# Layer 0 of a two-layer transformer: token tiles transposed by VectorE in 32x32 blocks, with rows regrouped by transfers

## The chip, the core and the metric

The program runs on one core of a Trainium2 chip. The core has five engines that run their own instruction queues in order and wait for each other through semaphores: TensorE (PE; its weight loads are shown as PEld), VectorE (DVE), ScalarE (ACT), GpSimd (POOL) and SyncE (SP), which here only issues DMA transfers. Matrix products read from SBUF, the on-chip memory of 128 partitions, and write to PSUM, from where VectorE or ScalarE copies ("evacuates") them back to SBUF. Sixteen DMA engines move data between DRAM and SBUF. The metric is the device time of one execution in microseconds (us).

## What is computed

Two layers on 1024 tokens of 512 channels, all in float32. Each layer is attention and a feed-forward product, each followed by adding its input and a layer normalisation:

```python
x = L0_attn_x                                      # (4, 256, 512)
x = _layernorm(x + _L0_attn_ref(x, Wq, bq, Wk, bk, Wv, bv, Wo, bo))
x = _layernorm(x + _L0_ffn_ref(x, q_scales, q_vals, bias))
x = _layernorm(x + _L1_attn_ref(x, w_qkv, w_o))
x = _layernorm(x + _L1_ffn_ref(x, kernel))
```

Layer 0 has 32 query heads of 16 channels on 8 key and value heads, 4 batches of 256 positions, causal; its feed-forward weight is quantised, `W = q_scales * (q_vals - 128)` in blocks of 32, and `out = x @ W.T + bias`. Layer 1 has 32 heads of 128 channels and a distance bias.

## The kernel before

The tokens lie in eight tiles of 128 rows (`tt` 0 to 7); a batch `b` is the tiles 2b and 2b+1. A matrix product needs the channels on the partitions, so each token tile is transposed before it is used: 128 tokens x 512 channels become `[128, 4, 128]`, channel within a group of 128, group `c`, token.

Layer 0 needs this three times for each tile: the input `x` (before the projections, `project0`), the normalised `x1` (before the feed-forward product `pf`) and the normalised `x2` (for layer 1, into `x2T`; both in `tail0`). `transposed` does it with four TensorE transposes into one PSUM bank (`pt_x`, line 272) and one copy out. `evacuate` gives the copies out of PSUM to VectorE (line 102) and ScalarE (line 104) in turns.

The softmax of layer 0 runs in 64 steps `(b, qt, h, i)`: 4 batches, 2 halves of the queries (128 each; the first sees 128 keys, the second 256), and 8 groups of 4 heads. `begin0` of a step computes scores into one of two PSUM banks (`sc`, line 484, pool `ps_s0`), adds the causal mask (VectorE, line 489), takes the negated maximum (`nm`, VectorE, line 492) and the four exponentials with their sums (ScalarE, line 276); `divided` multiplies by the reciprocal of the sums on GpSimd (line 284) one step later. `transpose0`, three steps later, transposes the probabilities on TensorE (`pt`, line 299); `end0` at the end of each half multiplies by the values (`o`, line 532) and starts a `tail0`.

`run` starts one step after another and calls `fill` in each. `fill` lets every open `tail0` go on to its next `yield` and lets the projections of the next batch go on by one piece. `tail0(tt)` is: output projection `py` (line 440), sum with the input, statistics, the normalisation to `x1` (line 266), some empty `yield`s, transpose of `x1`, `pf` (line 457), sum, statistics, normalisation to `x2`, empty `yield`s, transpose of `x2`. The framework has a scheduler: the instructions on each engine come out in an order that it plans, except where `keep_in_program_order` or `issue_after` hold them. What it planned is then fixed; on the chip each engine takes its instructions in that order.

All loads but three are issued by SP, in its queue's order: first those of batch 0 and the small ones, then input tiles 2 and 3, `bo_b`, the quantised weights `qv` (1 MB) and `qs`, `wop` in eight pieces, `fb_b`, tiles 4 to 7, `table`, and the first weights of layer 1 (`load_weights1`). Eight semaphores are used in turn, so a transfer is issued when the one eight before it has landed. `feed_forward_weight` dequantises `qv` on VectorE (line 210) and transposes it (`pw`).

After layer 0, `project1` begins layer 1 with products that need tiles 0 to 3 of `x2T` (`p_k`, `p_q`, `p_v`); `token_sums` on GpSimd (lines 606 to 609) needs tiles 0 to 2 and 4 to 6 first, then 3 and 7. The weights of `p_v` (2 MB, line 724) are loaded into memory that layer 0 used until its last `py`. In layer 1 a helper `transposed_by_blocks` is already there: VectorE transposes 32x32 blocks (line 310) and transfers through DRAM put the blocks in place (lines 316 and 320, tensor `way`). It is not changed.

Of the kernel before, what the change touches and what calls it, by code (L numbers as in the profile page):

```python
# [12 lines left out]
F32 = mybir.dt.float32  # L13
I32 = mybir.dt.int32
# [6 lines left out]
P = 128  # L21
B, S, D = 4, 256, 512
NTT = B * S // P
NC = D // P
# [37 lines left out]
def block_kernel(  # L62
# [20 lines left out]
    nc = tc.nc  # L83
    slopes = [float(s) for s in alibi_slopes()]

    def pool(stack, name, bufs=1, **kw):
        return stack.enter_context(tc.tile_pool(name=name, bufs=bufs, **kw))
# [3 lines left out]
    w1 = pool(ctx, "w1", 2)  # L91
    dram = pool(ctx, "dram", 4, space=bass.MemoryType.DRAM)

    turn = [0]
    last = []

    def evacuate(dst, src):

        if not last:
            turn[0] ^= 1  # L100
        if turn[0] and not last:
            nc.vector.tensor_copy(dst, src)
        else:
            nc.scalar.copy(dst, src)  # L104


    x = []
    xf = x_in.flatten_outer_dims()
# [10 lines left out]
    x2T = const.tile([P, NC, B * S], F32, name="x2T")  # L119
# [4 lines left out]
    wa = pool(la, "wa", side="right")  # L124
    a0 = pool(la, "a0", 2, side="right")
# [7 lines left out]
    def bank_t(name):  # L133
        return ring[0].tile([P, 4, P], F32, tag=ring[1], name=name)

    def bank_m(name):
        return ps_w.tile([P, D], F32, tag="w", name=name)
# [11 lines left out]
    bo_b = wa.tile([P, D], F32, name="bo_b")  # L149
    fb_b = w0.tile([P, D], F32, name="fb_b")  # L150
    brow = wa.tile([G + 1, P], F32, name="brow")
    qv = wa.tile([P, NC, D], I32, name="qv")
    qs = wa.tile([P, NC, D // BLK], F32, name="qs")
    wf_n = qv.bitcast(F32)

    tc.keep_in_program_order(nc.scalar.dma_start(wk, Wk.rearrange("(c p) n -> p c n", p=P)))
    tc.keep_in_program_order(
# [7 lines left out]
    nc.sync.dma_start(brow[G : G + 1, :], bk.unsqueeze(0))  # L165
    nc.sync.dma_start(wv, Wv.rearrange("(c p) n -> p c n", p=P))
    nc.sync.dma_start(bv_b, bv.partition_broadcast(P))
    for tt in range(2, 4):
        nc.sync.dma_start(x[tt], xf[ts(tt, P), :])
    nc.sync.dma_start(bo_b, bo.partition_broadcast(P))  # L170
    nc.sync.dma_start(qv, q_vals.rearrange("(c p) n k -> p c (n k)", p=P))
    nc.sync.dma_start(qs, q_scales.rearrange("(c p) n -> p c n", p=P))
# [1 line left out]
    for h in range(NKV):  # L174
        nc.sync.dma_start(wop[16 * h : 16 * h + 16, :, :], wo_v[h])
    nc.sync.dma_start(fb_b, f_bias.partition_broadcast(P))
    for tt in range(4, NTT):
        nc.sync.dma_start(x[tt], xf[ts(tt, P), :])
    nc.sync.dma_start(table, dist)

# [7 lines left out]
    def bias_columns():  # L188

        pt = bank_t("pt_bias")  # L190
        nc.tensor.transpose(pt[:, 0, 0 : G + 1], brow, ident[0 : G + 1, 0 : G + 1])
        nc.vector.tensor_copy(bcol, pt[:, 0, 0 : G + 1])
# [3 lines left out]
    def query_columns():  # L196

        for i in range(G):
            ins = (nc.vector.tensor_copy, nc.scalar.copy, nc.gpsimd.tensor_copy)[min(i, 2)](
                wq[:, :, i, :].rearrange("p c (h d) -> p c h d", d=16), wq_v[:, :, i]  # L200
            )
            tc.keep_in_program_order(ins)
# [23 lines left out]
    s0 = pool(l0, "s0", 2)  # L226
# [27 lines left out]
    def norm_factors(y, name):  # L254

        st = s0.tile([P, 6], F32, tag="bn", name=f"bn_{name}", bufs=4)
        mv = s0.tile([P, 2], F32, tag="mv", name=f"mv_{name}", bufs=4)
        rs = s0.tile([P, 1], F32, tag="rs", name=f"rs_{name}", bufs=4)
        nc.vector.bn_stats(st, y)
        nc.vector.bn_aggr(mv, st)  # L260
        nc.vector.tensor_scalar(rs, mv[:, 1:2], EPS, 1.0, ALU.add, ALU.mult)
        powers.append(nc.gpsimd.tensor_tensor(rs, rs, minus_half, ALU.pow))
        return mv[:, 0:1], rs

    def normalise(dst, y, factors):
        nc.vector.tensor_scalar(dst, y, *factors, ALU.subtract, ALU.mult)

    def transposed(dst, src, name):

        pt = bank_t(f"pt_{name}")  # L270
        for c in range(NC):
            nc.tensor.transpose(pt[:, c, :], src[:, ts(c, P)], ident)
        evacuate(dst, pt)

    def exponentials(pr, sc, nm, sums, i, w):
        nc.scalar.activation(  # L276
            pr[:, i, 0:w], sc, AF.Exp, bias=nm[:, i : i + 1], accum_out=sums[:, i : i + 1]
        )
# [91 lines left out]
    def project0(b):  # L370
        xT = a0.tile([P, NC, S], F32, tag="xT", name=f"xT_{b}", bufs=1)
        qT = a0.tile([P, G, S], F32, tag="qT", name=f"qT_{b}")
        kT = a0.tile([P, 2, S], F32, tag="kT", name=f"kT_{b}")
        v = a0.tile([P, 2, 4, 64], F32, tag="v", name=f"v_{b}")
        nc.gpsimd.memset(v, 0.0)
        qkv0[b] = (qT, kT, v)
        rest = ROOM[min(b, 2)]
        for _ in range(rest[0]):
            yield True
        for j in range(2):  # L380
            transposed(xT[:, :, ts(j, P)], x[2 * b + j], f"x_{b}_{j}")
        if b == 0:
            bias_columns()
            query_columns()
        yield True
        pk = bank_m(f"pk_{b}")
        for c in range(NC):
            nc.tensor.matmul(
                pk[:, 0:S], wk[:, c, :], xT[:, c, :], start=(c == 0), stop=(c == NC - 1)
            )  # L390
        for e in range(2):
            nc.vector.tensor_scalar(
                kT[:, e, :], pk[:, 0:S], bcol[:, G : G + 1], even[:, e : e + 1], ALU.add, ALU.mult
            )
        yield True
        for i in range(G):
            for _ in range(rest[1 + i]):
                yield True
            pq = bank_m(f"pq_{b}_{i}")
            for c in range(NC):  # L400
                nc.tensor.matmul(  # L401
                    pq[:, 0:S], wq[:, c, i, :], xT[:, c, :], start=(c == 0), stop=(c == NC - 1)
                )
            nc.vector.tensor_scalar(
                qT[:, i, :], pq[:, 0:S], bcol[:, i : i + 1], 0.25, ALU.add, ALU.mult
            )
            if i > 1:
                tt = 2 * b + i - 2
                tc.keep_in_program_order(nc.gpsimd.tensor_tensor(x[tt], x[tt], bo_b, ALU.add))
            yield True  # L410
        for _ in range(rest[5]):
            yield True
        pv = bank_m(f"pv_{b}")
        for j in range(2):
            for c in range(NC):
                nc.tensor.matmul(
                    pv[:, ts(j, P)],
                    xT[:, c, ts(j, P)],
                    wv[:, c, :],
                    start=(c == 0),  # L420
                    stop=(c == NC - 1),
                )
        for e in range(2):
            nc.vector.tensor_tensor(
                v[:, :, :, 48 * e : 48 * e + 16],
                pv[:, 0 : 2 * P].rearrange("p (j r e d) -> p j r e d", j=2, e=2, d=16)[:, :, :, e],
                bv_b.rearrange("p (r e d) -> p r e d", e=2, d=16)[:, :, e]
                .unsqueeze(1)
                .to_broadcast([P, 2, 4, 16]),
                ALU.add,  # L430
            )
        yield True

    x2 = {}

    def tail0(tt, oT):

        py = bank_m(f"py_{tt}")
        for i in range(G):
            nc.tensor.matmul(py, oT[:, i, :], wop[:, i, :], start=(i == 0), stop=(i == G - 1))  # L440
        y = s0.tile([P, D], F32, tag="y", name=f"y_{tt}")
        nc.vector.tensor_tensor(y, py, x[tt], ALU.add)
        factors = norm_factors(y, f"a{tt}")
        yield True
        x1 = s0.tile([P, D], F32, tag="x1", name=f"x1_{tt}")
        normalise(x1, y, factors)
        yield True
        if tt < NTT - 1:
            yield True
            yield True  # L450
        x1T = s0.tile([P, NC, P], F32, tag="x1T", name=f"x1T_{tt}")
        transposed(x1T, x1, f"x1_{tt}")
        nc.gpsimd.tensor_tensor(x1, x1, fb_b, ALU.add)
        yield True
        pf = bank_m(f"pf_{tt}")
        for c in range(NC):
            nc.tensor.matmul(  # L457
                pf, x1T[:, c, :], wfT[:, c, :], start=(c == 0), stop=(c == NC - 1)
            )
        y2 = s0.tile([P, D], F32, tag="y", name=f"y2_{tt}")  # L460
        nc.vector.tensor_tensor(y2, pf, x1, ALU.add)
        factors = norm_factors(y2, f"b{tt}")
        yield True
        x2[tt] = xp.tile([P, D], F32, tag="x", name=f"x2_{tt}")
        normalise(x2[tt], y2, factors)
        yield True
        if tt < NTT - 1:
            yield True
            yield True
        transposed(x2T[:, :, ts(tt, P)], x2[tt], f"x2_{tt}")  # L470
        yield True

    ahead, tails = deque(), deque()
# [82 lines left out]
    def fill():  # L556
        advance_all(tails)
        advance(ahead)

    ahead.append(project0(0))  # L560
    tails.append(feed_forward_weight())
    run(
# [7 lines left out]
        more=2,  # L570
        rest=divide0,
    )
    la.close()


# [527 lines left out]
```

## Time and profile before

| | us |
|---|---|
| median of 3 runs (lowest, highest) | 961.02 (960.78, 964.9) |
| the profiled execution, its own time | 960.96 |
| its span, first to last instruction | 958.8 |
| layer 0, its first score to its last `py` | about 14 to 270 |
| PE busy in the span | 922.0 (96%) |
| DVE busy | 619.4 (65%) |
| ACT busy | 315.2 (33%) |
| POOL busy | 445.6 (46%) |
| mean granted TensorE clock | 0.992 |

Busy time counts an engine's instructions from start to end. PE's instructions are pipelined, so one that lasts 0.6 us may hold the engine for less; the next one's start tells. "Idle" comes with a releaser: whose event ended the wait. Until 36 us the DMA engines are busy with the loads; after that they are idle until the weights of layer 1 are loaded at 270 us.

### The profile page before, as it was taken

How to read it: one execution, taken by the hardware profiler on the slowest of the kernel's cores; microseconds unless marked ns; L12 is line 12 of the kernel's file. 1: busy time of each engine (PE TensorE's matmuls, PEld its weight loads, DVE VectorE, ACT ScalarE, POOL GpSimd, SP SyncE). 2: the span in 40 equal slices, each digit the busy share in tenths (PEclk: the TensorE clock that was granted, in tenths of full speed). 3: DMA queues.
4: the chain of work that ended last, by engine and by line, in shares of the span. 5: the costliest groups of instructions: out<-in, count | busy, mean ns of one | idle time of the engine just before them, and what ended most of it. 6: DMA issues, size and time to landing. Idle time of an engine off the chain costs nothing.

```text
span 958.8 us, 11377 instructions
## 1 busy us (share of the span) xinstructions
PE 922.0 (96%) x3593; PEld 554.1 (58%) x3593; DVE 619.4 (65%) x1291; ACT 315.2 (33%) x1194; POOL 445.6 (46%) x461
## 2 busy tenths in 40 slices
PE   8999999998899999999999999999999999999996
PEld 5655455553544445666666666666666666666652
DVE  4886777778533447655667666666676576666566
ACT  3674555466411003232222222212122122214441
POOL 3563553554457015445443543534543534556732
PEclk9999999999899999999999999999999999999998
DMA  8500000000020102444443353343344333432001
GB/s 242 184 1 1 0 1 1 1 1 1 1 88 22 45 0 72 128 115 126 110 135 86 112 152 99 121 125 95 117 125 111 115 83 110 126 94 69 1 34 55
DMA packets 76418, 74.45 MB, mean 78 GB/s; under 512 B 5957, under 2 KB 52678, under 8 KB 76358
## 3 DMA queue, kind: packets, MB, share of 16 engines
q1 hardware_dynamic: 75014, 72.02, 26.2%
q10 hardware_dynamic: 1344, 1.70, 0.6%
q8 instruction: 29, 0.48, 0.2%
q14 instruction: 31, 0.25, 0.1%
HBM read 49.58 MB, written 24.12 MB: 77 GB/s over the span
## 4 chain that ended last, share of the span: by engine, by line
PE 79%; POOL 9%; DVE 6%; ACT 2%; issue 1%; DMA 1%; ACTq 0%; POOLq 0%; DVEq 0%
PE p_q L632 18%; PE po L881 14%; PE sc L968 7%; PE o L1008 7%; PE p_k L632 5%; PE p_v L632 5%; PE sc L484 4%; PE pt L299 3%; PE py L440 3%; PE pf L457 3%; PE o L532 2%; PE pq L401 2%; POOL pr L284 2%; ACT pr L276 2%; PE py L842 2%; POOL x L903 2%
## 5 line engine op out<-in xcount | busy, mean ns | idle before, releaser
L276 ACT ACTIVATE pr<-sc,nm 128x256 f32<-128x256 f32 (+1 forms) x512 | 209.5, 421 | 362.2 <-DVE nm L984 277.2
L284 POOL TENSOR_TENSOR pr<-pr,sums 128x512 f32<-128x512 f32 (+1 forms) x128 | 190.4, 1489 | 231.2 <-DVE sums L281 220.9
L976 DVE SCALAR_TENSOR_TENSOR sc<-table,sc 128x128 f32<-128x128 f32 (+1 forms) x256 | 86.1, 356 | 34.7 <-PE sc L968 32.4
L276 ACT ACTIVATION_READ_ACCUMULATOR pr<-sc,nm 128x1 f32 x512 | 104.2, 203 | 0.0
L968 PEld LDWEIGHTS sc<-kT,qT 128*128 128x128 f32 x512 | 82.3, 191 | 35.1 <-issue 29.7
L968 PE MATMUL sc<-kT,qT 128*128 128x256 f32 (+1 forms) x512 | 95.0, 327 | 0.0
L1008 PE MATMUL o<-prT,v 128*128 128x512 f32 x192 | 92.9, 592 | 0.0
L310 DVE STREAM_TRANSPOSE blocks<-pr 128x512 f32<-128x512 f32 x84 | 57.6, 698 | 45.2 <-POOL pr L284 45.1
L646 DVE TENSOR_TENSOR qT<-p_q,qT 128x512 f32<-128x512 f32 x96 | 64.6, 686 | 33.6 <-PE p_q L632 32.8
L299 PE MATMUL pt<-ident,pr 128*128 128x128 f32 x432 | 64.3, 284 | 11.7 <-POOL pr L284 8.2
L299 PEld LDWEIGHTS pt<-ident,pr 128*128 128x128 f32 x432 | 50.7, 145 | 38.1 <-issue 19.9
L984 DVE TENSOR_REDUCE nm<-sc 128x2 f32<-128x512 f32 (+1 forms) x128 | 70.1, 551 | 1.5
L484 PE MATMUL sc<-kT,qT 32*128 32x256 f32 (+1 forms) x256 | 61.6, 532 | 2.8 <-ACT pr L276 2.7
L492 DVE TENSOR_REDUCE nm<-sc 128x4 f32<-128x512 f32 (+1 forms) x64 | 61.0, 954 | 1.2
L881 PE MATMUL po<-wo,so 128*128 128x256 f32 x224 | 58.0, 381 | 2.1 <-POOL so L612 2.1
L632 PE MATMUL p_q<-x2T,ws_q 128*128 128x512 f32 x128 | 59.8, 592 | 0.0
L489 DVE TENSOR_TENSOR sc<-sc,causal 128x512 f32<-128x512 f32 x64 | 44.4, 694 | 22.8 <-PE sc L484 22.5
L104 ACT COPY o<-o 128x512 f32<-128x512 f32 x29 | 17.0, 586 | 124.9 <-PE o L1008 124.9
L632 PE MATMUL p_q<-xt,ws_q 128*128 128x512 f32 x128 | 57.7, 592 | 0.0
L881 PE MATMUL po<-wo,o 128*128 128x256 f32 x224 | 57.7, 380 | 0.0
L632 PE MATMUL p_q<-x2T,wq 128*128 128x512 f32 x128 | 57.6, 592 | 0.0
L881 PE MATMUL po<-to,so 128*128 128x256 f32 x224 | 53.3, 381 | 1.0 <-POOL so L615 1.0
(155 smaller groups left out, 1410.2 us busy)
## 6 DMA issues: line engine op xcount, KB each, us to landing
way<-blocks SPq DMA_DIRECT2D x112, 128.0 KB, 2.5
prT<-way SPq DMA_DIRECT2D x28, 512.0 KB, 3.7
wq<-in_L_attn_w_qkv_dram SPq DMA_DIRECT2D x8, 1024.0 KB, 5.1
wo<-in_L_attn_w_o_dram SPq DMA_DIRECT2D x8, 1024.0 KB, 5.1
way<-blocks SPq DMA_DIRECT2D x112, 64.0 KB, 1.8
prT<-way SPq DMA_DIRECT2D x28, 256.0 KB, 2.6
wk<-in_L_attn_w_qkv_dram SPq DMA_DIRECT2D x4, 512.0 KB, 4.1
wv<-in_L_attn_w_qkv_dram SPq DMA_DIRECT2D x2, 1024.0 KB, 6.3
```

The source lines that it names most:

```text
L276: nc.scalar.activation(pr[:, i, 0:w], sc, AF.Exp, bias=nm[:, i : i + 1], accum_out=sums[:, i : i + 1])
L284: nc.gpsimd.tensor_tensor(pr[:, :, 0:w], pr[:, :, 0:w], sums.unsqueeze(2).to_broadcast([P, G, w]), ALU.mult)
L299: nc.tensor.transpose(pt[:, i, :], pr[:, i, ts(kt, P)], ident)
L484: nc.tensor.matmul(sc[:, j, :, 0:w], qT[rows, i, ts(qt, P)], kT[rows, :, 0:w], start=True, stop=True)
L492: nc.vector.tensor_reduce(nm, scf[:, :, 0:w], AX.X, ALU.max, negate=True)
L632: nc.tensor.matmul(bank, fixed, moving, start=(c == 0), stop=(c == 1))
L646: add = lambda dst, a, b: nc.vector.tensor_tensor(dst, a, b, ALU.add)
L881: nc.tensor.matmul(bank[:, ts(n, HALF)], left[:, c, :], right[:, c, :], start=(c == 0), stop=(c == 1),)
L968: nc.tensor.matmul(sc[:, m, 0:w], qT[:, 2 * j + m, b * S + qt * P : b * S + (qt + 1) * P], kT[:, b * S : b * S + w], start=True, stop=True,)
L976: nc.vector.scalar_tensor_tensor(sc[:, m, 0:w], table[:, 2 * P - w :], slopes[kv * G + 2 * j + m], sc[:, m, 0:w], ALU.mult, ALU.add,)
L984: nc.vector.tensor_reduce(nm[:, 2 * j : 2 * j + 2], sc[:, :, 0:w], AX.X, ALU.max, negate=True)
L1008: nc.tensor.matmul(o, v1[:, 2 * b + kt, ts(kv, P)], prT[:, kt].rearrange("p j h q -> p h j q"), start=(kt == 0), stop=(kt == qt),)
```

## The change

In layer 0 twenty of the twenty-four token tiles are no longer transposed by TensorE. VectorE's `transpose` turns 32x32 blocks, each within 32 partitions, so the rows have to be regrouped first. `load_regrouped` reads a tile of 128 tokens from DRAM so that partition `32a + s` gets, for the tokens `4s` to `4s + 3` and the four channel groups, the 32 channels of its block `a`: four transfers, one for each `a`, each of 512 pieces of 32 floats (128 bytes). One `transpose` of the tile, written with a stride of four tokens, then gives the same layout as before.

- Input tiles: batch 0 stays on TensorE. For batches 1 to 3, `load_batch` loads both tiles regrouped from the input in DRAM (8 transfers): batch 1 where tiles 2 and 3 were loaded, batch 2 before the plain loads, batch 3 from within `project0(2)`. The plain tiles 2 to 7, still needed for the sum, are now all loaded after `fb_b`.
- `x1` and `x2` of tiles 0 to 6: `way_out` stores the tile to DRAM after its normalisation, `way_back` loads it regrouped into one buffer and transposes it. Tile 7 stays on TensorE.
- `evacuate`: in layer 0 one copy in three goes to VectorE, then every second one as before.
- `qv` takes a buffer of the layer 1 output weights, so the second of these (`wo`, 1 MB) is loaded later.

```diff
     turn = [0]
+    shares = [3]
     def evacuate(dst, src):
         if not last:
-            turn[0] ^= 1
-        if turn[0] and not last:
+            turn[0] += 1
+        if turn[0] % shares[0] == 1 and not last:
             nc.vector.tensor_copy(dst, src)
...
-    qv = wa.tile([P, NC, D], I32, name="qv")
+    wf_n = w1.tile([P, NC, D], F32, tag="wo1", name="wf_n")
+    qv = wf_n.bitcast(I32)
...
-    for tt in range(2, 4):
-        nc.sync.dma_start(x[tt], xf[ts(tt, P), :])
+    def load_regrouped(dst, src):
+        for a in range(4):
+            nc.sync.dma_start(
+                dst[ts(a, 32)].rearrange("s j c f -> s (j c) f"),
+                src.rearrange("(s j) (c a f) -> a s (j c) f", j=4, c=NC, f=32)[a],
+            )
+    def load_batch(b):
+        rows[b] = a0.tile([P, 8, NC, 32], F32, tag="rows", name=f"rows_{b}")
+        for j in range(2):
+            load_regrouped(rows[b][:, 4 * j : 4 * j + 4], xf[ts(2 * b + j, P), :])
+    load_batch(1)
     nc.sync.dma_start(bo_b, bo.partition_broadcast(P))
...
     nc.sync.dma_start(fb_b, f_bias.partition_broadcast(P))
-    for tt in range(4, NTT):
+    load_batch(2)
+    for tt in range(2, NTT):
         nc.sync.dma_start(x[tt], xf[ts(tt, P), :])
...
+    def transposed_regrouped(dst, src):
+        ins = nc.vector.transpose(dst.rearrange("p c (s j) -> p j c s", j=4), src)
+        tc.keep_in_program_order(ins)
+    def way_out(src, name):
+        way = dram.tile([P, D], F32, tag="rows", name=f"rows_{name}")
+        nc.sync.dma_start(way, src)
+        return way
+    def way_back(dst, way, name):
+        back = s0.tile([P, 4, NC, 32], F32, tag="back", name=f"back_{name}", bufs=1)
+        load_regrouped(back, way)
+        transposed_regrouped(dst, back)
...
         for j in range(2):
-            transposed(xT[:, :, ts(j, P)], x[2 * b + j], f"x_{b}_{j}")
+            if b == 0:
+                transposed(xT[:, :, ts(j, P)], x[j], f"x_{b}_{j}")
+            else:
+                transposed_regrouped(xT[:, :, ts(j, P)], rows[b][:, 4 * j : 4 * j + 4])
+        if b == 2:
+            load_batch(3)
...
         normalise(x1, y, factors)
-        yield True
         if tt < NTT - 1:
+            way = way_out(x1, f"x1_{tt}")
+        yield True
+        if tt < NTT - 1:
             yield True
             yield True
         x1T = s0.tile([P, NC, P], F32, tag="x1T", name=f"x1T_{tt}")
-        transposed(x1T, x1, f"x1_{tt}")
+        if tt < NTT - 1:
+            way_back(x1T, way, f"x1_{tt}")
+        else:
+            transposed(x1T, x1, f"x1_{tt}")
```

`x2` is changed as `x1` is, and `shares[0] = 2` follows the `run` of layer 0.

The scheduler's order moves with it. This is what TensorE has, in the program as built, in the first half and in the middle of batch 2. Each line is a score step `(b, qt, h, i)` and what stands between it and the next score; `pt` is one tile of probabilities, `pt_x` one token tile; part of a product is given as a share.

```
step       before                       after
2,0,0,0    pt pt pt_x                   pt pt pt pt
2,0,0,1    pt pt pf(1/4)                -
2,0,0,2    pf(3/4) pt_x pt_x pt         -
2,0,0,3    pt pk pt                     -
2,0,1,0    pt o                         pf pt pt
2,0,1,1    py pt                        o(7/16) pk pt pt o(9/16)
2,0,1,2    pt_x pq pt                   py pt pq pt
2,0,1,3    pq pt                        pq pt
2,1,0,0    pt                           pt
2,1,0,1    pt_x pt pf(1/4)              pt
2,1,0,2    pf(3/4) pq pt                -
2,1,0,3    pq pt pt                     pf pq pt pq pt pt
```

In batch 1 the first half has the same empty places, with one `pt` after step 1,0,0,1; in batch 3 `pf` comes after two scores in the first half and after step 3,1,0,3 in the second. On VectorE the transpose of `x1` stands directly in front of `pf`'s need: after the causal addition of the third bare step (2,0,0,3) in the first half, after the maximum of step 2,1,0,2 in the second.

More of the change, by code (lines that the diff above doesn't have):

```diff
@@ L151, in block_kernel @@
     brow = wa.tile([G + 1, P], F32, name="brow")
-    qv = wa.tile([P, NC, D], I32, name="qv")
+    wf_n = w1.tile([P, NC, D], F32, tag="wo1", name="wf_n")
+    qv = wf_n.bitcast(I32)
     qs = wa.tile([P, NC, D // BLK], F32, name="qs")
-    wf_n = qv.bitcast(F32)
     tc.keep_in_program_order(nc.scalar.dma_start(wk, Wk.rearrange("(c p) n -> p c n", p=P)))
@@ L167, in block_kernel @@
     nc.sync.dma_start(bv_b, bv.partition_broadcast(P))
-    for tt in range(2, 4):
-        nc.sync.dma_start(x[tt], xf[ts(tt, P), :])
+    rows = {}
+    def load_regrouped(dst, src):
[9 more added lines that the diff above has]
+    load_batch(1)
     nc.sync.dma_start(bo_b, bo.partition_broadcast(P))
@@ L465, in tail0 @@
         normalise(x2[tt], y2, factors)
+        if tt < NTT - 1:
+            way = way_out(x2[tt], f"x2_{tt}")
         yield True
@@ L469, in tail0 @@
             yield True
-        transposed(x2T[:, :, ts(tt, P)], x2[tt], f"x2_{tt}")
+        if tt < NTT - 1:
+            way_back(x2T[:, :, ts(tt, P)], way, f"x2_{tt}")
+        else:
+            transposed(x2T[:, :, ts(tt, P)], x2[tt], f"x2_{tt}")
         yield True
@@ L572, in block_kernel @@
     )
+    shares[0] = 2
     la.close()
```

## The prediction

> **What bounds the kernel now.** I read the busy time by stretch first, because the page's average (PE 96%) mixes two layers and the change touches one. The columns are the stretch and its length, busy us (instructions) of PE, PEld, DVE, ACT and POOL, the granted clock, the DMA share, GB/s.
>
> ```profile
> 10.00:70.00 60.00, 57.52 (x320) 37.34 (x318) 48.65 (x93) 37.39 (x153) 32.58 (x25) 1.00 0.42 129
> 70.00:136.00 66.00, 62.87 (x321) 35.23 (x320) 48.11 (x93) 35.41 (x143) 31.00 (x26) 0.97 0.00 1
> 136.00:202.00 66.00, 62.88 (x327) 35.19 (x326) 49.16 (x95) 37.02 (x150) 32.59 (x27) 1.00 0.00 1
> 202.00:270.00 68.00, 59.91 (x299) 29.76 (x300) 44.22 (x85) 34.05 (x134) 29.17 (x23) 0.95 0.00 1
> ```
>
> Layer 0 is four batches of some 66 us. TensorE is idle 2.5, 3.1, 3.1 and 8.1 us of them: it is the bound, but only because it has other work to put between the softmax steps. The transfers are idle after 36 us. The removed work is in the grouped lines (the shown window also holds tile 7 and batch 0, which stay); beside it is the layer 1 row nearest to what replaces it.
>
> ```profile
> L272 PE MATMUL pt_x<-ident,x 128*128 128x128 f32 x96 | 15.8, 299 | 4.2 <-DMA x<-in_L_attn_x_dram 4.2
> L310 DVE STREAM_TRANSPOSE blocks<-pr 128x512 f32<-128x512 f32 x84 | 57.6, 698 | 45.2 <-POOL pr L284 45.1
> ```
>
> Third, the chain of waits, for how fast a softmax step can go when TensorE has nothing else (start, us, what):
>
> ```profile
> 37.35 1.08 PE sc L484 x4
> ...
> 38.46 0.70 DVE sc L489
> ...
> 39.75 1.13 DVE nm L492
> ...
> 40.98 1.94 ACT pr L276 x8
> ...
> 42.96 1.12 PE sc L484 x3
> ```
>
> The scores have two PSUM banks, so a score waits for the exponentials of the step two before it: at 42.96 it starts 0.04 us after them. A round of a 256-wide step is 1.08 + 0.70 + 1.13 + 1.94 and hand-overs, some 5 us for two steps. A 128-wide one is 0.63 + 0.70 + 0.69 + 1.41 + 0.3 = 3.7 us.
>
> Fourth, how TensorE fills such a place now (batch 2, second half):
>
> ```profile
> 161.78 1.13 PE L484 MATMUL sc<-kT,qT 32*128 32x512 f32 x4
> 162.84 0.66 PE L299 MATMUL pt<-ident,pr 128*128 128x128 f32 x4
> 163.43 1.13 PE L484 MATMUL sc<-kT,qT 32*128 32x512 f32 x4
> 164.49 0.66 PE L272 MATMUL pt_x<-ident,x 128*128 128x128 f32 x4
> 164.98 0.60 PE L299 MATMUL pt<-ident,pr 128*128 128x128 f32 x4
> 166.33 1.10 PE L457 MATMUL pf<-wfT,x1T 128*128 128x512 f32 x2 [0.75 <-DVE x1T L102]
> 167.35 1.13 PE L484 MATMUL sc<-kT,qT 32*128 32x512 f32 x4
> 168.41 2.84 PE L457 MATMUL pf<-wfT,x1T 128*128 128x512 f32 x6
> ```
>
> The feed-forward product pf (L457) begins before the third score and fills the wait behind it; all idle in the stretch is 0.75 us.
>
> **What it removes.** Twenty tiles of four PE transposes (x2 to x7 of the input, x1 and x2 of tiles 0 to 6). A tile holds TensorE from its start to the next start: 164.49 to 164.98 is 0.49 us, others 0.44; I take 0.47, so 9.4 us, with 8.8 below and, by busy time (12.79 us for these 80 between 30 and 330 us), 12.8 above. The Trainium skill weighs against the change here: "VectorE: DVE Perf Modes", The three transpose paths, gives TensorE 390 ns and VectorE 311 ns for a 128x128 bf16 block and advises TensorE where PSUM will do. By the page's figure, an estimate, 80 transposes would be worth 31 us; the trace, where they overlap, gives 0.12 us each, and I go by the trace.
>
> Twenty PSUM copies go too. The share of one in three gives VectorE 26 of the 76 left instead of 43 of 96, and 20 stream transposes: 26 x 0.68 + 20 x 0.70 = 31.7 us for 29.2. ScalarE keeps 50 for 53. VectorE idles a quarter of layer 0, which hides 2.5 us; without that cover it is the cost. No row shows a transpose that writes every fourth word; between 0.66 us (the plain copies) and twice the 0.70, I take 0.70.
>
> **What it adds in transfers.** A round trip is one store and four loads, each of 512 pieces of 128 bytes: 128 pieces for each of 16 DMA engines. No row has such pieces in bulk; the nearest are the 512-byte ones of way<-blocks. In the window 374 to 380 us they are
>
> ```profile
> q1 hardware_dynamic: 1096, 0.54, 41.1%
> ```
>
> so 0.411 x 6 us x 16 / 1096 = 36 ns a packet. There four issues of 64 pieces an engine took 374.63 to 378.70 us: 2.3 us of packets and 1.8 us of fixed time. So the trip is 2.0 (the out_dram<-yo store, 256 KB) + 1.8 + 128 x 0.036 = 8.4 us. Bounds: a quarter of the packet time if only bytes counted (5.0 us for the trip), twice it if short pieces cost more (13 us). I take 36 ns, the nearest row. The Trainium skill, "DMA: Bandwidth & Descriptors", Specifications, says that under 512 bytes a transfer falls from line rate into read-modify-write; no run here shows it, and it would put the trip at the upper bound.
>
> The trip must fit between the normalisation and the place where VectorE's in-order queue reaches the transpose; the order as built and the times of now give 9.5 us (x2 of tile 0), 11.5 (x1 of tile 1), 11.8, 8.5, 10.6 and 10.5 for the tightest, more for the rest. At 8.4 us all are covered: 0. At 13 us six are late by 3.4, 1.5, 1.2, 4.5, 2.4 and 2.5 us, and what waits behind them on VectorE is the causal addition and the maxima, for which ScalarE and then the next score wait: 15.5 us. Tile 0's first trip has 2 MB of layer 1 weights put ahead of its loads: normalised at 60.7 us, + 2.0 + 5.6 (2 MB at 375 GB/s) + 6.4 = 74.7, due at about 75.9; 0, or 3 if those take their 5.1 us each. GpSimd's addition of the bias to x1 now also waits for the store, 2 us, long before its present 67.63. SP issues 94 more transfers at 0.45 us in a queue that waits idle for 244 us.
>
> At the start the rows of batch 1 cost 256 x 0.036 = 9.2 us of all DMA engines instead of 1.4, ahead of the quantised weights, which land at 18.4 now, so at 26.2. VectorE first uses them at 27.03: hidden by 0.8 us; at twice the packet time they are 8.4 us late. The rows of batch 2 add 9.2, so input tile 2 lands near 44 and is wanted near 57: hidden.
>
> **What it moves.** This decides. In the order as built, pf waits for the transpose on VectorE and stands behind it, and nothing fills the scores before it. Batch 2, first half, from the end of score (2,0,0,1): its three followers stand alone, then pf. (2,0,0,0) ended 2.4 us earlier, but a PSUM copy waits between its causal addition and its maximum, so its exponentials end at +1.0; the scores then start at 1.0, 2.9 and 4.5, and pf at 5.1. TensorE has 1.9 us of work in that: 3.2 idle against 0.5 now (0.34 and the like), + 2.7. Batch 1 has one transpose instead of four in front: pf at 7.1 with 2.1 us of work, 5.0 against 0.7, + 4.3. Batch 3 has two scores, + 0.7. Second half of batch 2, from the end of (2,1,0,0): the next scores begin at 0.44, 4.45 and 6.3; VectorE's transpose follows the maximum of the second of them, and pf starts at 8.0. Idle 2.3 + 0.8 + 0.75 = 3.9 against the 0.75 shown, + 3.1; the same for batch 1. In batch 3 TensorE already waits 1.62, 1.34 and 0.61 us around there, so + 1.5. Together + 15.4. No row has a bare stretch, so the bounds are 0 (the loops far enough ahead) and 20 (ScalarE's 0.59 us copies, now two of three, falling between).
>
> At the layer's end, SP puts the fourth load of the last trip behind the 2 MB of value weights, which wait, as now, for the last py:
>
> ```profile
> SPq L724 <- PE py L440: 244.4, 1, 244.4
> ```
>
> That is at 270.3; so it lands near 279 and x2T of tile 6 is there 5 us later than now (274.6). GpSimd's token sums and the PSUM banks behind VectorE pass on 1.5 us (0 to 4); the early products on TensorE hide the rest.
>
> With the softmax ahead after each bare stretch, some of today's small waits go: - 1.5 (0 to 3).
>
> **Sum.** - 9.4 + 15.4 + 1.5 - 1.5 = + 6.0 us. The profiled execution took 960.96 us (span 958.8 and 2.2 around it), 0.06 below the median 961.02, so 967.0 us either way. No change that can be told means within 0.5%, 4.8 us.
>
> **The rivals.** (a) It gets faster: the score banks are free when TensorE comes to the bare stretches, because the softmax ran ahead during the longer products in front. For it: VectorE and ScalarE idle a quarter and more. Against it: nothing of the order shown is long enough in front of batch 1's. Price: - 9.4 + 1.5 = 953 us; it decides once the added idle is under 3.1 us (with the small waits kept). (b) The two sides cancel: added idle between 4.6 and 14 us with the rest as above, 961. (c) Short pieces cost twice: 8.4 at the start, 15.5 at the trips: 991. Against it: nothing but the nearest row. (d) It doesn't do what it says: the freed TensorE time only becomes waiting for the softmax, and nothing is added: 961, part of (b).
>
> **Chances.** The forecast, slower by the bare stretches, 0.50; (a) 0.17; (b) and (d) 0.23; (c) 0.10. So faster 0.17, within 0.5% 0.23, slower 0.60. The likeliest case's own range is 962 to 975; the range for 8 in 10 is 954 to 980, which leaves out the lower part of (a) and (c).
>
> **What would show it.** L272 has 16 transposes left in layer 0. PE's busy time falls by about 10 us while the stretch from 10 us to the first layer 1 product grows. The idle in front of pf, released by VectorE's transpose or by ACT pr, rises from 1.5 us to 10 or more. The loads of back land 6 to 7 us after their first issue, and VectorE waits for DMA under 2 us in all. It would be wrong if pf's matmuls start right behind another product, or if the waits that grow are on DMA.

## The result, and the profile after

The changed kernel takes 1011.23 us (median of 4 runs, 1008.46 to 1013.39) beside 962.83 us for the kernel before on the same chip: a ratio of 1.0509, 95% interval 1.0478 to 1.054. It is slower by some 48 us where 6 were forecast, and it lies far outside the range of 954 to 980. The profiled execution took 1010.42 us, its span is 1008.6 (before: 958.8).

The pages of before and of the changed kernel, busy time of the engines, then the granted clock in 40 slices:

```profile
PE 922.0 (96%) x3593; PEld 554.1 (58%) x3593; DVE 619.4 (65%) x1291; ACT 315.2 (33%) x1194; POOL 445.6 (46%) x461
...
PEclk9999999999899999999999999999999999999998
```

```profile
PE 942.5 (93%) x3513; PEld 557.9 (55%) x3513; DVE 626.1 (62%) x1283; ACT 319.3 (32%) x1202; POOL 443.9 (44%) x461
...
PEclk9896897898698999999999999999999999999998
```

Read the first lines against each other: 80 transposes are gone (3513 matmuls for 3593), and yet PE is busy 20.5 us longer. The clock lines say why. In the changed kernel the first 13 slices are layer 0, and only five of them have a clock of 90% or more; before, one slice of layer 0 was below that. Layer 1 runs as it did: from the first product of `p_v` to the end it takes 674.4 us, and 674.2 before. The same matmuls of layer 0 take longer.

The stretch around tile 1's `x1` in slices of 3.41 us (the length is explained below); columns: stretch and length, busy us (instructions) of PE, PEld, DVE, ACT and POOL, granted clock, DMA share, GB/s:

```profile
64.00:67.41 3.41, 3.41 (x26) 2.60 (x25) 1.66 (x5) 0.80 (x2) 2.74 (x3) 1.00 0.00 0
67.41:70.83 3.42, 2.72 (x18) 1.52 (x16) 3.39 (x7) 1.52 (x7) 1.39 (x1) 1.00 0.73 216
70.83:74.24 3.41, 2.07 (x14) 1.14 (x12) 3.20 (x6) 3.41 (x10) 3.41 (x3) 1.00 1.02 383
74.24:77.65 3.41, 3.17 (x12) 1.94 (x12) 1.69 (x4) 3.10 (x14) 2.08 (x2) 0.50 1.05 208
77.65:81.06 3.41, 2.48 (x9) 1.00 (x8) 2.13 (x5) 2.51 (x12) 1.42 (x2) 0.50 0.61 96
81.06:84.48 3.42, 1.26 (x6) 0.51 (x4) 2.54 (x5) 2.53 (x14) 1.70 (x2) 0.50 0.15 26
84.48:87.89 3.41, 2.75 (x4) 1.20 (x5) 1.17 (x3) 1.50 (x8) 1.04 (x1) 0.50 0.00 0
87.89:91.30 3.41, 3.41 (x6) 1.34 (x5) 0.00 (x0) 0.00 (x0) 0.00 (x0) 0.50 0.00 0
91.30:94.72 3.42, 3.18 (x24) 1.89 (x26) 2.69 (x7) 0.58 (x1) 0.00 (x0) 1.00 0.00 0
```

From 70.83 to 74.24 TensorE is busy 2.07 of 3.41 us, 61%. Its idle there is three short waits: for exponentials, for ScalarE's copy of probabilities and for GpSimd's probabilities. Before, a transpose of `x` and the first quarter of `pf` stood in this place. In the next slice its clock is half, and it stays so for five slices, until one slice (87.89) is busy throughout. In these five TensorE is busy 13.07 us; at full clock the same work would take about half of that. The chain of waits at the end of it (start, us, what):

```profile
82.14 1.25 PE sc L532 x4
...
84.02 1.08 DVE x1T L293
...
85.14 6.75 PE pf L500 x8
```

This is the bare stretch of the prediction, with `pf` standing behind VectorE's transpose. But its eight matmuls take 6.75 us; the eight of `py`, of the same shape, take 3.71 at full clock (308.16 in a list further down).

The rest is read from TensorE's waits between 10 and 330 us (waited for: us in all, times, longest):

```profile
PE sc L532 <- ACT pr L309: 15.3, 14, 2.4
PE pt L332 <- POOL pr L317: 9.2, 5, 3.4
PE p_q L681 <- DVE x2T L293: 5.5, 1, 5.5
PE pf L500 <- DVE x1T L293: 4.0, 4, 1.8
PE pt L332 <- DVE v L462: 3.2, 3, 1.5
...
PE pf L500 <- DVE sums L314: 0.9, 1, 0.9
```

Of before, the two that the prediction is about:

```profile
PE sc L484 <- ACT pr L276: 2.7, 5, 0.7
PE pf L457 <- DVE x1T L102: 1.5, 2, 0.7
```

The second of the list was 6.2 then, the fifth 0.2; the third and the last weren't there.

With the busy time of PE and the record of the clock, each span can be split in three: *work*, PE's busy time with that at half clock counted half; *clock loss*, the other half; *idle*, the rest (from 10 us to 8 us before the end of the span; us).

| | span | work | clock loss | idle | time at half clock |
|---|---|---|---|---|---|
| before | 958.8 | 910.8 | 4.6 | 25.4 | 10.2 in 2 stretches |
| after | 1008.6 | 902.3 | 33.8 | 54.5 | 81.9 in 9 stretches |
| difference | +49.8 | −8.5 | +29.2 | +29.1 | |

So the removed work did leave, and two losses of equal size came: TensorE idles 29 us more, and its slower clock costs another 29.

Where the time went: layer 1's first product (`p_k`) starts 41.8 us later (311.70 for 269.95), and from there to the end it is 8.0 us longer (696.9 for 688.9).

### The profile page after: what moved, and what is told of

It reads as the page before. It is cut to its first block, busy times and chain, and to the rows that moved or that the text cites. A ratio compares the mean times of both kernels' runs of the same rounds, so it can differ in the third digit from the quotient of the medians.

```text
span 1008.6 us, 11380 instructions
## 1 busy us (share of the span) xinstructions
PE 942.5 (93%) x3513; PEld 557.9 (55%) x3513; DVE 626.1 (62%) x1283; ACT 319.3 (32%) x1202; POOL 443.9 (44%) x461
## 4 chain that ended last, share of the span: by engine, by line
PE 75%; POOL 9%; DVE 8%; ACT 3%; issue 2%; DMA 2%; POOLq 0%; DVEq 0%; SPq 0%; ACTq 0%
PE p_q L681 18%; PE po L930 14%; PE sc L1017 7%; PE o L1057 7%; PE p_v L681 5%; PE p_k L681 4%; PE pf L500 4%; PE sc L532 4%; PE pq L439 3%; PE pt L332 3%; PE py L478 3%; POOL pr L317 2%; ACT pr L309 2%; PE py L891 2%; POOL x L952 2%
## 5 line engine op out<-in xcount | busy, mean ns | idle before, releaser
L532 PE MATMUL sc<-kT,qT 32*128 32x256 f32 (+1 forms) x256 | 72.2, 627 | 15.4 <-ACT pr L309 15.3
L681 PE MATMUL p_q<-x2T,wq 128*128 128x512 f32 x128 | 60.4, 615 | 5.5 <-DVE x2T L293 5.5
L105 ACT COPY prT<-pt 128x512 f32<-128x512 f32 x76 | 43.5, 594 | 63.5 <-PE pt L332 63.4
```

Of the source, the lines that this page charges most:

```text
L532: nc.tensor.matmul(sc[:, j, :, 0:w], qT[rows, i, ts(qt, P)], kT[rows, :, 0:w], start=True, stop=True)
L681: nc.tensor.matmul(bank, fixed, moving, start=(c == 0), stop=(c == 1))
```

## The experiments

Each version was timed at least four times, beside the kernel before on the same chip. All edits but those of e10 to e18 start from the changed kernel. Times that came back are differences of medians; the ratios and their 95% intervals say which are clear of noise.

**First, which part of the change.** Each of e1 to e4 undoes one.

```diff
 e1:  -  way_back(x1T, way, ...)           +  transposed(x1T, x1, ...)      # every tile; no way_out
 e2:  -  way_back(x2T[...], way, ...)      +  transposed(x2T[...], x2[tt], ...)
 e3:  -  load_batch(1), (2), (3)           +  x[2], x[3] loaded there, all x on transposed()
 e4:  -  shares = [3]                      +  shares = [2]
```

> x1 is transposed by TensorE again; x of batches 1 to 3 and x2 still take the new way, and the copy share stays at one in three. Theory (the wait for x1 leaves TensorE partly idle, its clock falls to half, and what follows runs at half clock): the runs of three or four score steps in front of pf are gone from TensorE's order, so the nine half-clock stretches (81.9 us in all after 10 us of the span) shrink to three or fewer, and the time is 972, 962 to 985. Rival, the transfers (each of the three tensors moved costs alike, 24, 28 and 28 loads of 64 KB): a third of 48 us comes back, 995. Rival, ScalarE's share of the copies: no change, 1005 to 1012.

> x2 is transposed by TensorE again; x of batches 1 to 3 and x1 still take the new way. Theory (wait for x1, half clock): one run of three score steps in front of pf is left in TensorE's order, and the late fourth load at the layer's end is gone (about 7 us there): 990, 980 to 1000. Rival, transfers alike: 995. Rival, ScalarE's share: 1005 to 1012.

> x of batches 1 to 3 is transposed by TensorE again and loaded as before; x1 and x2 still take the new way. Theory (wait for x1, half clock): the first run is there with four score steps and the one of batch 3 with three, one of the three runs is gone, and the late start (2.9 us) is gone: 998, 988 to 1006. Rival, transfers alike: 995. Rival, ScalarE's share: 1005 to 1012. If x alone is under 975, the loads of its pieces at the start and in front of the others were the cause.

> One PSUM copy in two goes to VectorE again in layer 0; everything else as in the changed kernel. Theory (wait for x1, half clock): the work that gates pf is as it was, the run of four score steps is gone from TensorE's order and the two of three are left: 1000, 990 to 1010. Rival, ScalarE's share: the loop from score to exponentials is what leaves TensorE idle, and it is ScalarE's two copies in three that make it long: 975 or less.

| | time, us | ratio to before | clock loss | idle |
|---|---|---|---|---|
| e1, x1 on TensorE | 984.37 | 1.0257 (1.0199 to 1.0314) | 22.9 | 39.2 |
| e2, x2 on TensorE | 1002.69 | 1.0443 (1.0401 to 1.0485) | 29.2 | 48.1 |
| e3, x on TensorE | 1000.36 | 1.0416 (1.0379 to 1.0454) | 31.1 | 48.8 |
| e4, share of two | 1006.24 | 1.0481 (1.0447 to 1.0516) | 37.4 | 51.8 |

`x1` is the largest part: 27 us came back, though my 972 was missed by 12. `x2` gave 8.5 (my 990 was missed as well), `x` 11, the share 5. By the ratios it is 24, 6, 9 and 3 us, and the intervals of e2 and e4 overlap that of the changed kernel (1.0478 to 1.054), so the 5 is not clear of noise. The three tensors take 24 to 28 small loads each, but `x1` gave two and a half times what the others did or more: the transfers by themselves are not the rule. ScalarE's share is refuted as the main cause.

**Then, what about `x1` and `x2`: the trip's time, the transfers, or the order.**

```diff
 e5:  -  way_back(x1T, way, ...)      +  way_back(dead, way, ...); transposed(x1T, x1, ...)     # x2 alike; x1T bufs=1
 e6:  -  store, load_regrouped(back)  +  transposed_regrouped(dst, src)                          # from the tile itself
 e7:     load_regrouped(back, way) moved from way_back to way_out; back bufs=2, x1T bufs=1
 e8:  +  tc.keep_in_program_order(...) around the matmuls of sc and of pf
```

> All of the changed kernel's new work is done, x1 and x2 stored, loaded in pieces and transposed by VectorE, but into a tile that nobody reads; TensorE transposes x1 and x2 as before, and nothing waits for the trips. x of batches 1 to 3 and the share of one in three stay as changed. Theory (the wait for x1's trip in front of pf): x and the share alone remain, which gave back 11 and 5 us when they were undone: 959 + 16 = 975, 965 to 985. Rival, the transfers and VectorE's added work cost by themselves: 995 or more.

> VectorE transposes x1 and x2 in 32x32 blocks straight from the tiles; they aren't stored and loaded, so the rows aren't regrouped (that part of the computation is left out, and pf and layer 1 work on blocks in another order). The removal of TensorE's transposes stays. Theory (the trip's time in front of pf): 975, 965 to 985. Rival, TensorE is idle because its transposes, which filled the gaps between score steps, are gone, whoever makes x1T: 995 or more, with half-clock stretches of 60 us or more.

> The four loads of a trip are issued right behind its store, three steps earlier than before; VectorE's transpose stays where it was (two buffers for back, one for x1T). Theory (the trip's time in front of pf): TensorE's order has a run of three score steps in front of pf twice where it had three, four and three; the wait shrinks and does not go: 990, 980 to 1000. Rivals, transfers by themselves, or the missing transposes: 1003 to 1012.

> The changed kernel with the score products and pf held in the program's order on TensorE, so that no score step is put in front of pf. Theory in the form that the order alone is at fault (score steps pulled ahead of pf): 975, 965 to 985. Theory in the form that the trip is too long for the place where pf stands: TensorE now waits in front of pf for VectorE's transpose of x1, seven times 2 to 4 us, and the time is 1000, 992 to 1015. Rival, transfers by themselves: 1003 to 1012.

| | time, us | ratio to before | clock loss | idle |
|---|---|---|---|---|
| e5, trips unread | 987.83 | 1.0275 (1.0228 to 1.0321) | 15.1 | 41.9 |
| e6, no trips | 996.46 | 1.0347 (1.0316 to 1.0379) | 29.4 | 46.6 |
| e7, early loads | 998.52 | 1.0375 (1.0341 to 1.0409) | 30.7 | 49.2 |
| e8, pinned order | 1010.27 | 1.0491 (1.0459 to 1.0524) | 33.3 | 59.0 |

My theory of the moment, that TensorE waits for the trip, fell with e6: without any store or load of `x1` and `x2`, 35 us of the loss remain, with 68.3 us at half clock; that is what the rival of the missing transposes said. e5 missed both of its forecasts: 987.83 lies between them. The trips are worth about 15, and e7 gets 13 by starting their loads earlier. About half of both is the layer's end: from the first `p_k` to the end it is 690.3 us in e6 and 690.2 in e7, and 696.9 in the changed kernel. e8 shows that score steps pulled ahead of `pf` are no cause of their own: held in order, TensorE waits 9.2 us for exponentials and 11.6 in front of `pf`, 20.8 together for 20.2.

In e6, TensorE's waits:

```profile
PE pt L329 <- POOL pr L314: 9.8, 7, 2.6
PE sc L529 <- ACT pr L306: 8.8, 8, 2.0
PE pf L497 <- DVE x1T L293: 3.9, 4, 1.8
```

`pf` still waits 3.9 us for VectorE's transpose, with no transfer in front of it.

**The clock, and the parts alone.** e9 gives TensorE work that nobody uses. e10 to e12 (and e18, below) make one part of the change alone. All of e10 to e18 keep the quantised weights in the buffer that the change gave them; no run undoes that by itself.

```diff
 e9:      pt = bank_t(...)
     +    for i in range(2):
     +        nc.tensor.transpose(pt[:, i, :], ident, ident)
          for i in range(G):
              nc.tensor.transpose(pt[:, i, :], pr[:, i, ts(kt, P)], ident)
```

> The changed kernel with two more transposes of the identity by TensorE in front of every group of four that transposes probabilities in layer 0, into the same PSUM tile, which the four then overwrite: 96 groups by two by 0.12 us, some 22 us of work for TensorE that nobody uses. Theory (a window of the clock in which TensorE is busy under about 0.6 brings at least one window of 3.4 us at half clock, and 33.8 us of the changed kernel are lost so): the loss falls to 15 us or less, and half of the added work lies in idle time: 1000, 985 to 1010, no slower than the changed kernel in spite of 22 us more work. Rival (the low clock follows the waits and costs nothing, since TensorE waits anyway): slower by half or more of the added work, 1021 to 1033.

> Only one PSUM copy in three on VectorE; x, x1 and x2 are transposed by TensorE in layer 0 as before the change. Undoing the share in the changed kernel gave back 5 us. Theory (the parts add up): 965, 960 to 970. Rival (the share costs only beside the trips, where ScalarE's loop bounds the steps): 958 to 962.

> Only x of batches 1 to 3 is loaded regrouped and transposed by VectorE; x1 and x2 on TensorE, one copy in two on VectorE. Theory (the parts add up): 970, 963 to 977, of it 3 us at the start. Rival (x costs only beside the trips, whose loads it delays): 960 to 965.

> Only x1 takes the trip; x and x2 on TensorE, one copy in two on VectorE. Theory (the parts add up, and x1 in front of pf is the largest): 986, 978 to 994. Rival (the trip of x1 costs so much only with TensorE already emptied by the others): 972 or less.

| | time, us | ratio to before | work | clock loss | idle |
|---|---|---|---|---|---|
| e9, after with filler | 1000.41 | 1.0391 (1.0364 to 1.0419) | 924.9 | 14.6 | 42.1 |
| e10, share alone | 972.75 | 1.013 (1.0064 to 1.0197) | 912.2 | 4.9 | 33.2 |
| e11, x alone | 966.19 | 1.0041 (1.0013 to 1.007) | 908.2 | 9.4 | 29.8 |
| e12, x1 alone | 997.81 | 1.0365 (1.0336 to 1.0394) | 907.6 | 27.5 | 41.8 |

e9 is the plainest of all. The page:

```profile
PE 946.3 (95%) x3729; PEld 572.7 (57%) x3729; DVE 625.8 (63%) x1283; ACT 320.5 (32%) x1202; POOL 444.3 (44%) x461
...
PEclk9998999999798999999999999999999999999998
```

By the split, TensorE does 22.6 us more work than in the changed kernel. Yet its time is 1000.41 against 1011.23. The clock loss falls by 19.2 us, and the idle time by 12.4. So the half clock is a price of its own, and not a sign of waiting that would be there anyway. One rival is left in e9: the filler also moved the scheduler's order a little. e15, below, settles it.

The share alone costs 10 us (I expected 5; the interval of its ratio allows 6 to 19), `x` alone 4 (10 expected), `x1` alone 35 (27 expected and gained by undoing it). With the 10 us of `x2` alone (e18) that is 59, where all together cost 48: the parts don't simply add up.

**Last, why `x1` costs so much without a trip.** All on `x1` alone: the place of VectorE's transpose, and TensorE's missing work.

```diff
 e13:     e12, with  transposed_regrouped(x1T, x1)  straight from the tile
 e14:     e13
     -    ins = nc.vector.transpose(...); tc.keep_in_program_order(ins)
     +    nc.vector.transpose(...)
 e15:     e13
     +    for c in range(NC): nc.tensor.transpose(pt[:, c, :], ident, ident)    # behind way_back, unread
 e16:     e12 with the lines of e15
 e17:     e14 with the lines of e15
 e18:     x2 alone takes the trip
```

> As with x1 alone (998, where before is 962), but VectorE transposes x1 straight from its tile, without store and loads (the rows are not regrouped, which part of the computation is left out). VectorE's transpose stands where it did, behind the maximum of the current score step and the reciprocal of the step before. Theory R (the trip's time): 970 or less. Theory P (the place: the reciprocal in front of the transpose waits for ScalarE's exponentials, so x1T and then pf come half a softmax loop late, trip or no trip): 988, 980 to 1000. Theory A (TensorE misses the 0.47 us of its own transposes, so its windows fall under the clock's limit): 985, 975 to 995.

> The same without the trip, and VectorE's transpose isn't held in the program's order, so that it stands right behind normalise, three steps earlier, and TensorE finds x1T ready. Theory P: 967, 960 to 973. Theory A: 985, 975 to 995, since TensorE's work is the same as in the run before.

> As the first of these, with four transposes of the identity by TensorE, unread, where x1 was transposed before (7 times 0.47 us). Theory A: 970, 962 to 977. Theory P: 988, 978 to 1000.

> x1 alone with its trip, and the same four unread transposes of the identity per tile. Theory A: 975, 965 to 985. Theory P and theory R: 998, 988 to 1006.

> x1 without the trip, VectorE's transpose free to stand three steps earlier, and four unread transposes of the identity by TensorE where x1 was transposed. If the place and TensorE's missing work are two separate losses of 6 us each: 974, 969 to 978. If both edits only lift the same windows over the clock's limit, the second brings nothing: 980, 978 to 985. If nothing else of x1's way costs anything, it is before's time: 960 to 966.

> Only x2 takes the trip; x and x1 on TensorE, one copy in two on VectorE. If the parts add up (undone in the changed kernel it gave back 8.5 us): 971, 966 to 976. If x2 costs only at the layer's end, where TensorE waits for the last piece behind a 2 MB load, 5.5 us in the changed kernel, less the 2.8 us of transposes removed: 965, 962 to 968. If it costs only beside the others: 962.

| | time, us | ratio to before | clock loss | idle |
|---|---|---|---|---|
| e13, no trip | 986.56 | 1.025 (1.0203 to 1.0296) | 26.2 | 37.3 |
| e14, no trip, transpose floats | 980.34 | 1.0201 (1.0149 to 1.0253) | 19.3 | 34.0 |
| e15, no trip, filler | 980.31 | 1.019 (1.0152 to 1.0227) | 15.8 | 33.8 |
| e16, trip, filler | 991.37 | 1.0301 (1.0256 to 1.0347) | 17.8 | 43.9 |
| e17, no trip, floats, filler | 975.79 | 1.0153 (1.0123 to 1.0183) | 12.9 | 30.9 |
| e18, x2 alone | 970.55 | 1.0102 (1.0073 to 1.013) | 9.8 | 34.5 |

No single theory holds: e14 missed what theory P said, e15 what theory A said. e13 to e15 and e17 leave the regrouping out, as e6 does. Taking the trip out gives 11 us (e12 to e13). Letting the transpose float gives 6 more (its interval overlaps that of e13), and so does the filler; both together give 11 of the 12, which lies in the range named for two separate losses. e13's and e14's `pf`, as groups (line, engine, operation, count; busy us, mean ns; idle before and its releaser):

```profile
L492 PE MATMUL pf<-wfT,x1T 128*128 128x512 f32 x56 | 39.6, 872 | 3.1 <-DVE x1T L293 3.1
```

```profile
L491 PE MATMUL pf<-wfT,x1T 128*128 128x512 f32 x56 | 35.1, 761 | 0.0
```

In e14 nothing waits for `x1T` any more; yet a `pf` matmul still takes 761 ns in the mean, where it took 621 before: 20 of 64 start at half clock, and 2 before. The wait is gone and the clock is still low (a loss of 19.3 us after 26.2). The filler lowers it without that: in e15 `pf` waits 3.0 us as in e13, and the clock loss is 15.8. Layer 0 of e15 has, by the names in the trace, every other instruction of TensorE, VectorE and ScalarE in the order of e13, so here the filler alone, and no other order, made the kernel faster. 15 us of `x1`'s 35 are left in e17, 8 of them clock loss and 5.5 idle. What sets them off (VectorE's 1.1 us within the softmax loop is one candidate) was not tried and stays open.

None of the versions beats the kernel before; the nearest is `x` alone.

## Why the prediction was wrong

- **The removed work** (−9.4): right. By the split it is 8.5 us. `pt_x` has 16 transposes left.
- **The bare stretches** (+15.4 of idle in front of `pf`): right in place and size. TensorE's waits for ScalarE's exponentials rose from 2.7 to 15.3 us, those of `pf` from 1.5 to 4.9: together +16.0. The sign for it that I had named, idle in front of `pf` up from 1.5 to 10 or more, came true. That the sum fits so well is in part luck: by place, TensorE waits 3.8 and 3.6 us in the two halves of batch 1 and 2.9 and 2.5 in those of batch 2, where 5.0, 3.9, 3.2 and 3.9 were worked out, and more than forecast in batch 3.
- **The step that failed is the sum itself.** It takes every matmul of layer 0 at the duration that it had before. There is no term for the granted clock, although the slices that I showed first have it: 0.97 and 0.95 in two of four. The emptied places leave TensorE busy for 61% (70.83), 33% (115.21) and 43% (190.3) of a clock window, and what follows, `pf` first of all, runs at half speed: 30 of its 64 matmuls start at half clock, 2 before. That is +29.2 us, more than half of the whole. The bare stretches came as I had said, and I priced only the idle in them. Nor are they the only place where the clock falls. At 115.21 and 190.3 the window that brings the fall holds a bare stretch (waits of 2.39 and 1.96 us for exponentials). At 152.7 and 289.3 it holds a wait for GpSimd's probabilities (2.02 and 3.42 us), at 70.83 the three short ones. At 70.83 and 152.7 the bare stretch comes later and only keeps the clock low (the slice at 81.06 is busy for 37%).
- **The layer's end** (+1.5, bounds 0 to 4): too small. The fourth load went behind the value weights as I had said; in the chain of waits (start, us, what):

```profile
308.16 3.71 PE py L478 x8
...
312.94 7.48 DMA back_x<-rows_x
...
320.55 1.09 DVE x2T L293
...
321.68 5.38 PE p_q L681 x6
```

  TensorE runs out of early products and waits 5.5 us, and two windows at half clock follow (from 319.99). e18 has the same wait (5.4) with `x2` alone, and e2, without `x2`'s trips, lacks it. In all, this end costs some 7 to 8 us: from the first `p_k` to the end of the span it is 696.5 to 698.8 us in the seven profiles in which `p_q` waits so for the late load (after, e1, e3, e4, e8, e9, e18), and 688.7 to 690.3 in the other thirteen. It is nearly all that `x2` alone costs: in e18 `p_k` starts at 270.10, and at 269.95 before.
- **The small waits** (−1.5): wrong in sign. TensorE's idle rose by 29.1 us in all; 16.0 and 5.5 of them are named above, so the other waits rose by some 7.6. Those of the probabilities' transposes for GpSimd (6.2 to 9.2) and behind `v` on VectorE (0.2 to 3.2) are most of it.
- **Taken at nothing, the trips:** in the right order for their length, wrong for their effect. From the page of after (issues, KB each, median us to landing):

```profile
rows_x<-x SPq DMA_DIRECT2D x14, 256.0 KB, 2.0
back_x<-rows_x SPq DMA_DIRECT2D x56, 64.0 KB, 2.5
```

  One trip's four loads were issued in 2.57 us (99.26 to 101.83), so with the store's 2.2 and the last load's 2.5 to 4.2 it is some 7 to 9 us, beside 8.4. The terms of that sum were wrong, though, and its fit is in part luck: from 258 to 263 us, with one trip's loads alone, 2112 packets take 33.6% of the 16 engines, so 0.336 x 5 us x 16 / 2112 = 12.7 ns a packet where 36 were taken. The pieces cost 3 us less than forecast, issue and landing more. VectorE waited for one trip only, 3.9 us, at the layer's end, where I had named under 2 us. So rival (c), short pieces at twice the price, is refuted. But without them 15 us came back (e6), and with trips that nobody waited for (and `x` and the share as changed) a loss of 26 was left (e5). How much of that is SP's queue, the scheduler's order, or GpSimd's wait for two of the stores (5.3 us) was not told apart.
- **Taken at nothing, the start:** the first score starts at 16.83 us instead of 13.91. The first `pq` starts 1.3 us later (11.97 for 10.69). In the ten profiles that load `rows` at the start it comes at 11.81 to 13.08, in the ten that don't at 10.68 to 11.37: that is these loads. The other 1.6 us are the clock: the first record of full speed is at 16.21 us (11.61 before), so `pq`'s first twelve matmuls take 4.93 us for 3.29. That varies with no load in the way: with the share alone it is at 14.76.
- **Taken at 0.70, VectorE's transposes:** they take 1.07 (`x1T`), 1.08 (`x2T`) and 1.10 us (`xT`) when they write every fourth word, within the bound of 1.4. Their price is 20 x 0.38 = 7.6 us of VectorE, in its queue between the softmax steps.
- **The other rivals:** (a) rested on the softmax being ahead. It wasn't: the first wait in the list above is the largest. (b) needed added idle between 4.6 and 14 us, and (d) none; it rose by 29.1.

## What to carry to other kernels

Before you take work away from TensorE, look how full it is in each window of its clock, not in the mean: in a window that is left 60% busy or less, the loss can be larger than the work that left, because what comes next runs at half speed. Here 8.5 us of work went, and the clock took 29. A product that is made to wait for another engine's transpose wants other matmuls in front of it in TensorE's own order; no run here tried that with useful work. And a filler of unread transposes, tried on the slow kernel, tells in one run whether the clock is part of a loss.

## What the runs showed of the hardware

**The clock can fall after a window that is partly busy; it need not be idle.** In the record of the clock of the twenty profiled executions, every stretch at half clock inside a span is a whole number of windows of 3.413 us (one to five). Of 48 windows at full clock in which TensorE was busy for less than 45%, all were followed by half clock; of 258 between 45 and 75%, 85 were; of 5059 above 75%, one. Back to full it went after none of 78 windows that were busy for less than 80%, and after 117 of 142 that were busy for 95% or more. The kernel before stood at the edge: its window at 110.6 us was busy for 59% and its clock fell, the ones at 219.8 and 223.2 us were busy for 63 and 62%, and it did not. The busy share alone does not decide between 45 and 75%: a window of before at 878.6 us was busy for 47% and kept its clock. What else does stays open.

The Trainium skill, "TensorE: Matmul & The Clock Gate", What's actually happening, has the two speeds and a free-running window of about 3.4 us, and this case's record agrees. It has the fall after an idle window; here the measurement decides, and a window that is busy for 61% was enough.

**Busy time at half clock.** The page's busy share counts slow matmuls as work: by the split, the changed kernel's 942.5 us (93%) hold 33.8 us that the clock added.
